# Rows and banks of the state-space stage clear of the last FP4 MLP, and six slots left to the scheduler

## The chip, the cores and the metric

One Trainium2 chip, of which the kernel uses one core. A core has five engines with a queue of instructions each: PE (TensorE, matrix products; its weight loads are told apart as PEld), DVE (VectorE), ACT (ScalarE), POOL (GpSimd) and SP (SyncE, which here issues transfers). They share the on-chip memory SBUF (128 partitions) and the accumulators PSUM (eight banks of 128 x 512 f32). The metric is device time of one launch in microseconds; lower is better.

## The reference

Eight layers, each `x = x + layer(norm(x))`, in four stages of one kernel. Around the change lie the FP4 MLP that ends the first stage and the state-space layers that follow it:

```python
def fp4_quant_dequant(x):           # blocks of 16 along the last dim
    scale = jnp.maximum(jnp.max(jnp.abs(xb), axis=-1, keepdims=True) / 6.0, 1e-12)
    idx = jnp.searchsorted(_MID, jnp.abs(xb / scale))
    q = _GRID[idx] * jnp.sign(xn) * scale
...
gate = fp4_linear(x, w_gate)        # [.., 128] x [352, 128]
y = fp4_linear(x, w_up)
h = jax.nn.silu(gate) * y
return fp4_linear(h, w_down)
```

```python
def mamba_block(x, Wi, cw, cb, Wx, Wdt, bdt, Alog, Dp, Wo):    # 4 layers
    xs, z = jnp.split(x @ Wi.T, 2, axis=-1)
    u = jax.nn.silu(conv(xs, cw) + cb)                        # 4 taps, causal
    dt, Bc, Cc = jnp.split(u @ Wx.T, [8, 24], axis=-1)
    dt = jax.nn.softplus(dt @ Wdt.T + bdt)
    def step(h, inp):                                         # over 256 positions
        dA = jnp.exp(dt_t[:, :, None] * A)                    # 256 channels x 16 states
        h = dA * h + dt_t[:, :, None] * B_t[:, None, :] * u_t[:, :, None]
        y = jnp.einsum('bds,bs->bd', h, C_t)
    ...
    return ((y + u * Dp) * jax.nn.silu(z)) @ Wo.T
```

The 2048 tokens (8 sequences of 256) are worked on in four blocks of 512.

## The kernel before

**Stage l0** runs spiking attention and the FP4 MLP for token blocks 0 to 3, with parts of different blocks woven together. The order of PE's instructions there is the order written in the program; the other engines' order is set by the framework's scheduler. PSUM is cut into banks by use: `mm` 0 to 3, `acc` 4 and 5, `ffn` 6 and 7. SBUF tiles come from pools, of which `fpool` (l0_f) holds the tiles of the MLP and `epool` (l0_e) those of attention's exponentials.

`mlp(tb, lo, hi, kind)` does the token columns lo to hi of a block: quantize the normed input into `xq` (`fp4`: L521 block maxima, L522 and L524 to L525 scale and its inverse, L527 divide, L531 and L532 the exponent's power of two, L534 and L536 rounding by adding and taking off a large number, L538 multiply by the scale; all on DVE, all tiles in SBUF), transpose (L265 on PE, copied by ACT at L268), multiply by gate and up (L722, L729), silu (L725, ACT), product into `h` (L730), quantize `h` into `hq` with the same lines, transpose in three pieces into `hT`, multiply by down (L743) and add to `x` (L746). The last block's MLP is run as two halves side by side, the second seven steps behind the first. The second half's names end in `_2` in the program (the profile cuts numbers off: both are `hq_l0f`, `d_l0f` and so on). It uses the banks of kind `mm`, the first those of kind `ffn`.

**Stage l1a** is the state-space stage. One job is one token block of one layer (4 x 4 jobs), one slot is one of the 16 states of a job: 256 slots. For a slot s:

- `spread` (L995, SP): a DMA that broadcasts two rows of B, or of C, from DRAM to all partitions (512 KB).
- `inflow` (L1001, POOL): `st = du * B row`.
- `decay` (L1007, ACT): `da = exp(dt * A)` into one of two PSUM tiles da0, da1; two instructions a slot.
- `scan` (L1012, DVE): the recurrence along the tokens, `da` from PSUM, `st` in place.
- odd slots: `turn`, four PE transposes (L1021) for each half and on DVE L1028 (slot 1: ACT, L1026) the product with C and the sum into `yt`; even slots: `weigh` (L1034, POOL), `st *= C row`, and a sum on PE (L1043). Slot 8 goes the way of the odd ones.

`front(job)` makes a job's inputs: norm's statistics on DVE (L872, L874) and POOL (L881 to L888), scaled by ACT (L893), transposed (L898), convolution (L909, then L914, silu L917), `xd` (L924, L927), dt (L938, L941, L942), the softplus (L948, L954), z (L964, L966) and DVE's L973 to L976, whose running operand is in PSUM. Its ACT steps switch between function tables (1.28 us a load). `norm(xs[3])` with L238, L240, L246 to L251 and L257 makes `y3`, the last block's input; it needs L746 of both halves.

Job 0's front, the norms and the first part of the job-1 front are given to l0's last steps as `following`. When l0 closes, its pools are freed and l1a's pools are opened in their place: `big` (the rows and the `st` tiles), `pool`, and in PSUM `mm` and `acc` with one bank each, da0, da1 (two banks each) and the sums `y` (two banks). A tile that lies where an older one lay waits for the older one's last reader.

All slots run in a loop `for g in range(len(slots) + 10)` in a `manual_schedule` of PE, DVE, ACT and POOL: these engines take the instructions in the order in which the loop issues them. SP's queue is in order too: the first `spread` holds up all later ones. The code ahead of the loop clears da0 and da1 (L1090, DVE), issues the first rows, three inflows and the first decay.

Of the kernel before, what the change touches and what calls it, by code (L numbers as in the profile page):

```python
# [174 lines left out]
def network_kernel(ctx: ExitStack, tc: tile.TileContext, x_in, packs, places, conv_w, out, stages=STAGES):  # L175
# [16 lines left out]
    def mm_tile(name, kind="mm"):  # L192
        return banks[kind].tile([P, TB], F32, tag=kind, name=name)
# [346 lines left out]
    def l0(w, following):  # L540
        with ExitStack() as es:
# [148 lines left out]
                    A.copy(wT[name], ps[:, :I0P])  # L690
                    yield

            def mlp(tb, lo=0, hi=NT, kind="ffn"):

                n = f"l0f{tb}" + (f"_{lo}" if lo else "")
                more = "2" if lo else ""
                part = range(lo, hi)
                x = xs[tb]

                def whole(tag, shape):  # L700
                    if (tb, tag) not in shared:
                        shared[tb, tag] = fpool.tile(shape, F32, tag=tag, name=f"{tag}_{n}")
                    return shared[tb, tag]

                room = lambda m: flat(whole("q_p", [P, NT, I0P])[:, lo:hi])[:, : (hi - lo) * m]
                if lo == 0:
                    shared[tb, "xn"] = layer_norm(x, n)
                xn = shared[tb, "xn"]
                yield
                xq = whole("xq", [P, NT, D])[:, lo:hi]  # L710
                yield from fp4(fpool, flat(xn[:, lo:hi]), flat(xq), (hi - lo) * D, f"x{n}", room(D), more)
                yield
                yield
                xqT = transposed(xq, n, kind=kind)
                yield
                yield
                h = whole("h", [P, NT, I0P])
                G.memset(h[:, lo:hi, I0:], 0.0)
                g = whole("g", [P, NT, I0])
                for i in part:  # L720
                    pg = mm_tile(f"g_{n}_{i}", kind)
                    T.matmul(pg[:, :I0], xqT[:, ts(i - lo)], wT["gate"][:, :I0], start=True, stop=True)  # L722
                    A.copy(g[:, i, :], pg[:, :I0])
                    yield
                A.activation(g[:, lo:hi], g[:, lo:hi], AF.Silu)  # L725
                yield
                for i in part:
                    pu = mm_tile(f"u_{n}_{i}", kind)
                    T.matmul(pu[:, :I0], xqT[:, ts(i - lo)], wT["up"][:, :I0], start=True, stop=True)  # L729
                    V.tensor_tensor(h[:, i, :I0], g[:, i, :], pu[:, :I0], ALU.mult)  # L730
                    yield
                hq = whole("hq", [P, NT, I0P])[:, lo:hi]
                yield from fp4(fpool, flat(h[:, lo:hi]), flat(hq), (hi - lo) * I0P, f"h{n}", room(I0P), more)
                yield
                yield
                hT = whole("hT", [P, 3, TB])
                for c in range(3):
                    transposed(hq[:, :, ts(c)], f"{n}_{c}", hT[:, c, lo * P : hi * P], kind=kind)
                    yield
                ps = mm_tile(f"d_{n}", kind)  # L740
                for i in part:
                    for c in range(3):
                        T.matmul(ps[:, ts(i)], hT[:, c, ts(i)], wT["down"][:, ts(c)], start=c == 0, stop=c == 2)  # L743
                    yield
                to = flat(x[:, lo:hi])
                V.tensor_tensor(to, to, ps[:, lo * P : hi * P], ALU.add)  # L746
# [28 lines left out]
            with tc.manual_schedule(engines={mybir.EngineType.PE}):  # L775
                for tb in range(2):
                    skip(normal(tb), 4)

                first_half = skip(currents(0), 4 + 10 + 8)
                rest = {}  # L780
                for tb in range(NTB + 1):
                    parts = []
                    if tb < NTB:

                        rest[tb] = attention(tb)
                        parts.append((take(rest[tb], 2 * H), 2 * H + 1))
                    if tb == 0:
                        parts.append((chain(first_half, currents(1), normal(2)), 18 + 40 + 4))
                        parts.append((weights(), 24))
                    elif tb < NTB:  # L790
                        ahead = [currents(tb + 1)] if tb + 1 < NTB else []
                        ahead += [normal(tb + 2)] if tb + 2 < NTB else []
                        if ahead:
                            parts.append((chain(*ahead), 40 + 4))
                    if tb == NTB:
                        last = beside(mlp(tb - 1, 0, NT // 2), mlp(tb - 1, NT // 2, NT, "mm"), 7)
                        parts.append((chain(rest[tb - 1], project(tb - 1), last), 7 + 5 + 36))
                    elif tb:
                        parts.append((chain(rest[tb - 1], project(tb - 1), mlp(tb - 1)), 7 + 5 + 37))

                    if tb >= NTB - 1:
                        n = 2 + 40 + 1 if tb < NTB else 2 + 2 + 1
                        parts.append((take(following, n), n + 1))
                    woven(*parts)


    def l1a(w0):
# [10 lines left out]
        with ExitStack() as es:  # L818
# [215 lines left out]
                G.tensor_tensor(st, st, row.unsqueeze(1).to_broadcast([P, 2, TB]), ALU.mult)  # L1034

            def open_sum(job):
                job.yacc = pda.tile([P, 2, TB], F32, tag="y", name=f"y_{job.n}")
                for c in range(2):
                    T.matmul(job.yacc[:, c, :], diags[job.l][:, c, :], job.u[:, c, :], start=True, stop=False)

# [43 lines left out]
            big = es.enter_context(tc.tile_pool(name="l1a_b", bufs=5))  # L1084
            pool = es.enter_context(tc.tile_pool(name="l1a", bufs=1))
            pda = es.enter_context(tc.tile_pool(name="l1a_da", bufs=1, space=bass.MemoryType.PSUM))

            for j in range(2):
                t = pda.tile([P, 2, TB], F32, tag=f"da{j}", name=f"da{j}")
# [33 lines left out]
                    adds[g - s + ADD[s]] = job, s  # L1123
            gens = {"norm": norm(xs[NTB - 1], f"l1a{NTB - 1}", ys[NTB - 1], gap=3)}
            step = lambda what: next(gens.get(what, iter(())), None)

            kinds = mybir.EngineType
            with tc.manual_schedule(engines={kinds.PE, kinds.DVE, kinds.Activation, kinds.Pool}):
                for g in range(len(slots) + 10):
                    job, s = slot(g)  # L1130

                    nxt = slot(g + LEAD)
                    if nxt[0] and nxt[1] == 0:
                        fronts.append(front(nxt[0]))
                    for gen in fronts:
                        next(gen, None)
                    if job:
                        if s == 0:
                            job.yt = pool.tile([P, NT, DI], F32, tag="yt", name=f"yt_{job.n}", bufs=2)
                            if job.tb == 2 and job.l + 1 < NL:  # L1140
                                gens["weights"] = layer_weights(job.l + 1)

                        rows_of(g + 3 * Q)
                        rows_from(g + 2 * Q)
                    nxt = slot(g + 1)
                    if nxt[0]:
                        decay(*nxt)
                    if slot(g + AHEAD)[0]:
                        inflow(*slot(g + AHEAD))
                    if job:  # L1150
                        scan(job, s)
                    for lag in (1, 2):
                        j2, s2 = slot(g - lag)
                        if j2 and s2 % 2:
                            turn(j2, s2, lag - 1)
                    j2, s2 = slot(g - 2)
                    if j2 and s2 in ADD:
                        weigh(j2, s2)
                    at = g % DS
                    if at in EXTRA:  # L1160
                        j2 = slot(g - DS * EXTRA[at][0])[0]
                        if j2:
                            turn(j2, *EXTRA[at][1:], "mm")
                    if at == 7:
                        step("tail")
                    if job and s == 8:
                        open_sum(job)
                    if g in adds:
                        add_up(*adds[g])
                    for gen in fronts:  # L1170
                        next(gen, None)
                    step("weights")
                    step("norm")
                    if at == 2 and slot(g - DS)[0]:
                        gens["tail"] = tail(slot(g - DS)[0])
                    if 2 < at < 7:
                        step("tail")
                    if g == len(slots) - 1:
                        gate(job.k)

# [440 lines left out]
```

## Time and profile before

| | |
|---|---|
| three runs | 2043.93, 2045.22, 2050.58 us; median 2045.22 |
| the profiled execution | 2052.19 us, its span 2050.4 us |
| busy, share of the span | PE 78%, DVE 79%, POOL 62%, ACT 53%, PE weight loads 46% |
| granted TensorE clock | 0.876 |
| L1012 scans, DVE | 256, 581.5 us, 2277 ns each |
| L1001 inflows, POOL | 256, 597.4 us, 2356 ns each |
| L1034 weighing, POOL | 112, 263.8 us, 2356 ns each |
| L1007 decays, ACT | 512, 351.2 us, 689 ns each |

The state-space stage lies between about 364 and 1345 us. The profile gives times from the start of the span. In the timelines a line is a start, a duration, the engine, the line of the code, the operation, out<-in, and in brackets the idle time before it with what ended it; neighbours of one kind are put together (x4), and their duration runs from the first's start to the last's end. A slice by stage gives each engine's busy time in a stretch. The profiled execution is 6.97 us above the median of the runs.

DVE's waits in the stage (400 to 1330 us): `da` from ACT 35.9 us in 26 waits, L1021 from PE 11.2, L1034 from POOL 2.2. POOL's longest single wait there is the one ahead of the first inflow, 21.43 us.

### The profile page before, as it was taken

The numbers are of one execution on the slowest core, as the hardware profiler recorded it, in microseconds if no ns is written. First come the engines' busy times: TensorE is split into PE (matmuls) and PEld (weight loads), VectorE is DVE, ScalarE is ACT, GpSimd is POOL, SyncE is SP. The second block draws the span as 40 slices with busy tenths as digits, with TensorE's granted clock in tenths as the row PEclk, the third lists the DMA queues.
The fourth block names the chain that finished last, engine by engine and source line by source line (L and its number), as shares of the span: only waits on it lengthen the run. The fifth ranks groups of instructions, "written<-read, shape, count | busy, mean of one in ns | idle before, by whom it ended". The sixth has DMA issues, their size and how long they took to land. (4 is left out here: it accounts for less than half of the span.)

```text
span 2050.4 us, 21148 instructions
## 1 busy us (share of the span) xinstructions
PE 1589.3 (78%) x6829; PEld 947.1 (46%) x6829; DVE 1630.0 (79%) x3009; ACT 1077.4 (53%) x1764; POOL 1266.7 (62%) x920
## 2 busy tenths in 40 slices
PE   4989895587777778877778777789999776794775
PEld 1434443244444444444444343444446575683665
DVE  6775546799999999999999999925655666899996
ACT  2654452676577776667676666522222243463442
POOL 2000101999899998999989999902343545836446
PEclk8999997699888998888898888899999988796887
DMA  4000001433223332233323333100022344220000
GB/s 129 1 1 1 1 2 58 145 107 134 93 105 120 111 125 94 103 115 105 119 103 112 100 112 105 62 1 0 1 74 98 111 150 130 65 72 9 6 6 6
DMA packets 67693, 153.27 MB, mean 75 GB/s; under 512 B 5248, under 2 KB 26368, under 8 KB 67328
## 3 DMA queue, kind: packets, MB, share of 16 engines
q1 hardware_dynamic: 60224, 123.79, 17.9%
q0 software_dynamic: 7360, 28.14, 4.2%
q8 instruction: 54, 0.88, 0.2%
q14 instruction: 55, 0.45, 0.1%
HBM read 142.74 MB, written 9.18 MB: 74 GB/s over the span
## 5 line engine op out<-in xcount | busy, mean ns | idle before, releaser
L1012 DVE TENSOR_TENSOR_SCAN st_l1a<-da,st_l1a 128x1024 f32<-128x1024 f32 x256 | 581.5, 2277 | 49.7 <-ACT da L1007 43.9
L1001 POOL TENSOR_TENSOR st_l1a<-du_l1a,b_l1a 128x1024 f32<-128x1024 f32 x256 | 597.4, 2356 | 21.4 <-DMA b_l1a<-rows_l1a 21.4
L1007 ACT ACTIVATE da<-dt_l1a,na 128x510 f32<-128x510 f32 x512 | 351.2, 689 | 112.9 <-DVE st_l1a L1012 104.2
L1021 PE MATMUL tr_l1a<-w_const,st_l1a 128*128 128x128 f32 x1152 | 201.0, 306 | 185.6 <-DVE yt_l1a L1028 164.2
L1021 PEld LDWEIGHTS tr_l1a<-w_const,st_l1a 128*128 128x128 f32 x1152 | 149.8, 157 | 331.9 <-issue 212.5
L1034 POOL TENSOR_TENSOR st_l1a<-st_l1a,c_l1a 128x1024 f32<-128x1024 f32 x112 | 263.8, 2356 | 60.5 <-DVE st_l1a L1012 60.5
L1043 PE MATMUL y_l1a<-st_l1a,w_const 128*128 128x512 f32 x448 | 243.9, 673 | 0.0
L1028 DVE SCALAR_TENSOR_TENSOR yt_l1a<-tr_l1a,ct_l1a,yt_l1a 128x256 f32<-128x256 f32 x512 | 215.6, 466 | 13.1 <-PE tr_l1a L1021 12.9
L628 PE MATMUL o_l0a<-ex_l0a,va_l0a 128*32 128x256 f32 x512 | 140.6, 401 | 1.9 <-ACT ex_l0a L620 1.9
L909 PE MATMUL u_l1a<-xp,cw 128*128 128x512 f32 x256 | 120.5, 594 | 1.7 <-ACT xp L901 0.9
L1043 PEld LDWEIGHTS y_l1a<-st_l1a,w_const 128*128 128x128 f32 x448 | 88.5, 220 | 66.0 <-issue 66.0
L1235 PE MATMUL h_l1f<-h_l1f,w_l1f 128*128 128x512 f32 x256 | 116.7, 593 | 0.0
L620 ACT ACTIVATE ex_l0a<-s_l0a 128x512 f32<-128x512 f32 x128 | 75.3, 595 | 73.8 <-PE s_l0a L615 73.5
L1508 POOL TENSOR_TENSOR xd<-de,ex_l3f 128x1024 f32<-128x1024 f32 x32 | 65.2, 2056 | 61.1 <-ACT de L1503 61.1
L1543 PE MATMUL wT<-w_const,wa 128*128 128x128 f32 x512 | 73.4, 312 | 22.6 <-ACT wa L1524 17.0
L1239 ACT ACTIVATE h_l1f<-h_l1f,w_l1f 128x512 f32<-128x512 f32 x32 | 22.0, 687 | 120.9 <-PE h_l1f L1235 120.9
L1543 PEld LDWEIGHTS wT<-w_const,wa 128*128 128x128 f32 x512 | 71.1, 226 | 23.9 <-ACT wa L1524 17.4
L1291 POOL TENSOR_TENSOR st_l2a<-st_l2a,qk_l2a 128x512 f32<-128x512 f32 x32 | 40.4, 1268 | 63.1 <-DVE st_l2a L1290 53.6
L1510 POOL TENSOR_TENSOR xd<-xd,ey_l3f 128x1024 f32<-128x1024 f32 x32 | 78.6, 2475 | 0.2
L1235 PEld LDWEIGHTS h_l1f<-h_l1f,w_l1f 128*128 128x128 f32 x256 | 48.6, 190 | 60.2 <-issue 59.2
L386 POOL DMA_INDIRECT we_l2f<-w_l2f,rows_l2f x44 | 45.5, 1034 | 48.5 <-PE y_l2f L419 31.3
L628 PEld LDWEIGHTS o_l0a<-ex_l0a,va_l0a 128*32 128x32 f32 x512 | 47.1, 113 | 59.9 <-issue 34.4
(490 smaller groups left out, 3260.9 us busy)
## 6 DMA issues: line engine op xcount, KB each, us to landing
b_l1a<-rows_l1a SPq DMA_DIRECT2D x128, 512.0 KB, 3.6
c_l1a<-rows_l1a SPq DMA_DIRECT2D x64, 512.0 KB, 4.1
w_l1f<-w_l1f SPq DMA_DIRECT2D x1, 2888.0 KB
in_l2f<-zero SPq DMA_DIRECT2D x4, 704.0 KB, 7.1
w_l1a<-w_l1a SPq DMA_DIRECT2D x4, 572.0 KB, 5.3
cw<-conv_w SPq DMA_DIRECT2D x4, 512.0 KB
xt_l2f<-in_l2f SPq DMA_DIRECT2D x8, 256.0 KB
out_l2f<-yt_l2f SPq DMA_DIRECT2D x8, 256.0 KB, 3.3
```

The costliest lines, as they stand in the source:

```text
L628: T.matmul(po[b, g][32 * j : 32 * j + 32, :S], va[:, 2 * b + kc, h, :], ex[:, ts(kc, S)], start=kc == 0, stop=kc == 1)
L909: T.matmul(seq(ps), cw[:, j, ts(c)], xp[:, :, j : j + S], start=j == 0, stop=j == 3)
L1001: G.tensor_tensor(t, job.du, row.unsqueeze(1).to_broadcast([P, 2, TB]), ALU.mult)
L1007: A.activation(seq(da[:, c, :])[:, :, 1:], seq(job.dt[:, c, :])[:, :, 1:], AF.Exp, scale=rates[job.l][:, k : k + 1])
L1012: V.tensor_tensor_scan(st, flat(das[s % 2]), st, 0.0, ALU.mult, ALU.add)
L1021: T.transpose(ps[:, j * DI + c * P : j * DI + (c + 1) * P], st[:, c, ts(i)], ident)
L1028: V.scalar_tensor_tensor(dst, src, cs, dst, ALU.mult, ALU.add)
L1034: G.tensor_tensor(st, st, row.unsqueeze(1).to_broadcast([P, 2, TB]), ALU.mult)
L1043: T.matmul(job.yacc[:, c, :], ident, job.st[s][:, c, :], start=False, stop=False)
L1235: T.matmul(ps, w(wn)[:, k * HID + c * P : k * HID + (c + 1) * P], h[:, k, :], start=k == 0, stop=k == NC - 1)
L1510: G.tensor_tensor(xd, xd, wide(ey[:, rs].unsqueeze(2), 2, NX, NK), ALU.mult)
L1543: T.matmul(ps[:, ts(c)], wa[:, h, ts(c)], ident, start=h == 0, stop=h == NH - 1)
```

## The change

The second half of the last MLP takes its PSUM tiles from `ffn` instead of `mm`, so both halves share banks 6 and 7. The tile `xq` moves from `fpool` to `epool` (one buffer). The sums `y` get a PSUM pool `py` of their own, opened after `pda`. The loop's body becomes a function `issue(g)`; it is called for slots 0 to 5 ahead of the `manual_schedule` and for the others in it.

```diff
-            def mlp(tb, lo=0, hi=NT, kind="ffn"):
+            def mlp(tb, lo=0, hi=NT):
...
-                def whole(tag, shape):
+                def whole(tag, shape, pool=fpool):
                     if (tb, tag) not in shared:
-                        shared[tb, tag] = fpool.tile(shape, F32, tag=tag, name=f"{tag}_{n}")
+                        shared[tb, tag] = pool.tile(shape, F32, tag=tag, name=f"{tag}_{n}", bufs=1)
                     return shared[tb, tag]
...
-                xq = whole("xq", [P, NT, D])[:, lo:hi]
+                xq = whole("xq", [P, NT, D], epool)[:, lo:hi]
...
-                xqT = transposed(xq, n, kind=kind)
+                xqT = transposed(xq, n, kind="ffn")
...
-                        last = beside(mlp(tb - 1, 0, NT // 2), mlp(tb - 1, NT // 2, NT, "mm"), 7)
+                        last = beside(mlp(tb - 1, 0, NT // 2), mlp(tb - 1, NT // 2, NT), 7)
...
-                job.yacc = pda.tile([P, 2, TB], F32, tag="y", name=f"y_{job.n}")
+                job.yacc = py.tile([P, 2, TB], F32, tag="y", name=f"y_{job.n}")
...
             pda = es.enter_context(tc.tile_pool(name="l1a_da", bufs=1, space=bass.MemoryType.PSUM))
+            py = es.enter_context(tc.tile_pool(name="l1a_py", bufs=1, space=bass.MemoryType.PSUM))
...
+            def issue(g):
+                job, s = slot(g)
+                ...
+
+            for g in range(6):
+                issue(g)
 
             kinds = mybir.EngineType
             with tc.manual_schedule(engines={kinds.PE, kinds.DVE, kinds.Activation, kinds.Pool}):
-                for g in range(len(slots) + 10):
-                    job, s = slot(g)
-                    ...
+                for g in range(6, len(slots) + 10):
+                    issue(g)
```

In the built program this orders the instructions of the boundary so:

- SP: the first row waits for L538 of the second half's `xq`, the transposes of `xq` on PE (L265), the last exponential of attention on ACT and an old POOL instruction. Before, it waited for L538 of `hq`, the last down product (L743), the last copy into `hT` (L268) and POOL's memset (L718).
- DVE: memsets of da and the statistics come ahead of L677; after L522 of the second half stand scan 0, L538 of the first half, L524, scan 1, L525, L527, scan 2, L531, L746 of the first half, L532, L238, L534, L238, L536, two L240, L538, scans 3 to 5, L746 of the second half, scan 6, two L238 and two L240, three pairs of L1028, L872 and L874 of block 2, four L257 of `y3`, scan 7. From scan 7 on the order is that of before.
- POOL: inflows 0 to 5, L1034 of slot 0, inflows 6 to 8, L1034 of slot 2, inflow 9, L1034 of slot 4, inflows 10 and 11, L1034 of slot 6, L246 to L251 for `y3`, inflow 12.
- ACT: silu of job 0's z (L984, with a table load on each side) stands among attention's last exponentials; the decays of slots 0 and 1 ahead of the MLP's first L268; three of the four L893 of job 1 ahead of the second half's L268 of `xq`; the decays of slots 2 to 6 among the copies into `hT`; after the last of these, L914, L1026, L914, L917, L927, L941 and L942 twice, L948, L951, L954, L966 in a row, and then the decay of slot 7.
- PE: one transpose of job 1 (L898) ahead of the second half's transposes of `xq`; the first convolution (L909) ahead of the transposes of `hq`; L1021 of slot 1 among the down products; the second convolution after the last down product, then L924, L938, L947 and L964 with L1021 of slots 3 and 5 between them.

More of the change, by code (lines that the diff above doesn't have):

```diff
@@ L720, in mlp @@
                 for i in part:
-                    pg = mm_tile(f"g_{n}_{i}", kind)
+                    pg = mm_tile(f"g_{n}_{i}", "ffn")
                     T.matmul(pg[:, :I0], xqT[:, ts(i - lo)], wT["gate"][:, :I0], start=True, stop=True)
@@ L727, in mlp @@
                 for i in part:
-                    pu = mm_tile(f"u_{n}_{i}", kind)
+                    pu = mm_tile(f"u_{n}_{i}", "ffn")
                     T.matmul(pu[:, :I0], xqT[:, ts(i - lo)], wT["up"][:, :I0], start=True, stop=True)
@@ L737, in mlp @@
                 for c in range(3):
-                    transposed(hq[:, :, ts(c)], f"{n}_{c}", hT[:, c, lo * P : hi * P], kind=kind)
+                    transposed(hq[:, :, ts(c)], f"{n}_{c}", hT[:, c, lo * P : hi * P], kind="ffn")
                     yield
-                ps = mm_tile(f"d_{n}", kind)
+                ps = mm_tile(f"d_{n}", "ffn")
                 for i in part:
@@ L1125, in l1a @@
             step = lambda what: next(gens.get(what, iter(())), None)
+            def issue(g):
+                job, s = slot(g)
+                nxt = slot(g + LEAD)
+                if nxt[0] and nxt[1] == 0:
+                    fronts.append(front(nxt[0]))
+                for gen in fronts:
+                    next(gen, None)
+                if job:
+                    if s == 0:
+                        job.yt = pool.tile([P, NT, DI], F32, tag="yt", name=f"yt_{job.n}", bufs=2)
+                        if job.tb == 2 and job.l + 1 < NL:
+                            gens["weights"] = layer_weights(job.l + 1)
+                    rows_of(g + 3 * Q)
+                    rows_from(g + 2 * Q)
+                nxt = slot(g + 1)
+                if nxt[0]:
+                    decay(*nxt)
+                if slot(g + AHEAD)[0]:
+                    inflow(*slot(g + AHEAD))
+                if job:
+                    scan(job, s)
+                for lag in (1, 2):
+                    j2, s2 = slot(g - lag)
+                    if j2 and s2 % 2:
+                        turn(j2, s2, lag - 1)
+                j2, s2 = slot(g - 2)
+                if j2 and s2 in ADD:
+                    weigh(j2, s2)
+                at = g % DS
+                if at in EXTRA:
+                    j2 = slot(g - DS * EXTRA[at][0])[0]
+                    if j2:
+                        turn(j2, *EXTRA[at][1:], "mm")
+                if at == 7:
+                    step("tail")
+                if job and s == 8:
+                    open_sum(job)
+                if g in adds:
+                    add_up(*adds[g])
+                for gen in fronts:
+                    next(gen, None)
+                step("weights")
+                step("norm")
+                if at == 2 and slot(g - DS)[0]:
+                    gens["tail"] = tail(slot(g - DS)[0])
+                if 2 < at < 7:
+                    step("tail")
+                if g == len(slots) - 1:
+                    gate(job.k)
@@ L1127, in l1a @@
+            for g in range(6):
+                issue(g)
             kinds = mybir.EngineType
             with tc.manual_schedule(engines={kinds.PE, kinds.DVE, kinds.Activation, kinds.Pool}):
-                for g in range(len(slots) + 10):
-                    job, s = slot(g)
[L1132 to L1179, printed above, removed]
```

## The prediction

> **What bounds the kernel now.** I read the busy shares first, then the slices by stage, then the timelines of VectorE (DVE), GpSimd (POOL) and SyncE's queue around the end of the FP4 MLP, where the change acts. Columns of the slices: the stretch, its length, busy time of PE, PE weight load, DVE, ACT and POOL with their instruction counts, granted clock, DMA share, GB/s.
>
> ```profile
> 333.00:358.00 25.00, 14.51 (x54) 9.94 (x54) 17.20 (x38) 8.39 (x19) 4.42 (x13) 0.71 0.00 0
> 364.00:388.00 24.00, 17.87 (x38) 6.87 (x38) 15.74 (x18) 19.36 (x30) 23.51 (x17) 0.65 0.45 148
> 388.00:402.00 14.00, 4.52 (x11) 2.10 (x10) 14.00 (x18) 7.50 (x10) 14.00 (x7) 0.50 0.34 118
> 402.00:420.00 18.00, 10.72 (x28) 5.77 (x29) 17.79 (x23) 8.84 (x15) 12.86 (x13) 0.72 0.26 88
> 420.00:500.00 80.00, 66.09 (x243) 35.62 (x242) 75.91 (x87) 53.33 (x79) 75.77 (x41) 0.91 0.34 114
> ```
>
> From 388 us on DVE is busy in 14.00 of 14, 17.79 of 18 and 75.91 of 80 us: the 256 slots of the state-space layers run at DVE's pace until about 1345 us. A shift of one slot is therefore carried to the end of the program, unless the 4.1 us idle in the last row take some of it up. The change can win only ahead of slot 7: from 333 to 388 DVE idles for 7.8 us (25.00 less 17.20), 3.9 (358 to 364) and 8.3 (24.00 less 15.74), 20 us in all. That is the ceiling.
>
> ```profile
> 354.24 0.95 DVE L538 TENSOR_TENSOR hq_l0f<-hq_l0f,sc_hl0f 128x768 f32<-128x768 f32 x1
> 357.99 1.28 SPq L995 DMA_DIRECT2D b_l1a<-rows_l1a  x3
> 361.87 13.88 POOL L1001 TENSOR_TENSOR st_l1a<-du_l1a,b_l1a 128x1024 f32<-128x1024 f32 x6 [21.43 <-DMA b_l1a<-rows_l1a]
> 392.40 9.04 DVE L257 TENSOR_SCALAR y<-x,mv_l1a,rs_l1a 128x128 f32<-128x128 f32 x4
> 401.37 2.28 DVE L1012 TENSOR_TENSOR_SCAN st_l1a<-da,st_l1a 128x1024 f32<-128x1024 f32 x1
> ```
>
> These are starts and durations. The MLP's last quantizing product ends at 355.19. The first row transfer is issued at 357.99, after the last down product, since its tile lies where the MLP's were; the first inflow follows 3.88 us later, with POOL idle 21.43 us before it. The line at 401.37 is the scan of slot 7 (slots 0 to 6 start at 364.25, 370.25, 376.30, 378.5, 381.98, 385.40, 388.38).
>
> **What the change moves.** Four edits have one answer, an earlier start: xq out of the MLP's pool, the second half on the banks of the first, a pool of its own for the sums, and the memsets of da ahead. The first row now waits only for the second half's transposes of xq.
>
> - That half is itself later. PE's queue has job 1's transposes ahead of xq's, and these need ACT's L893, which waits for POOL's chain ending at 340.43. Three L893 (1.26 us together) give 341.7, xq's two transposes (0.38) 342.2. So the copy that started at 338.36 moves to 342.5, and the second half's L730 from 343.52 to 345.65: +2.1 us.
> - The row goes out at about 342.25 instead of 357.99; the first inflow starts at 342.25 + 3.88 = 346.1, 15.8 us earlier. The 2888 KB weight load ahead on SP was issued at some 320 and does not compete; before, no DMA moved between 333 and 358.
> - Two memsets (1.82 us) go to about 319, beside ACT's exponentials; da of slots 0 and 1 fills ACT's 13.57 us of idle time before 332.73. The silu of z goes to about 306, with one more table load (1.28 us), and delays the chain to L677 by some 0.7 us, which I leave out; were it not hidden among the exponentials, it would cost 1.04 + 1.28 + 1.28 = 3.6 us.
>
> If nothing else changed, DVE would run the MLP's remainder and three scans together from 345.65: two L730 1.04, L521 0.95, L532 to L538 of the first half 0.56 + 0.96 + 0.96 + 0.89, L522 to L538 of the second 0.19 + 0.44 + 0.17 + 0.96 + 0.56 + 0.56 + 0.96 + 0.96 + 0.95, L746 0.42, statistics 0.63, scans 3 x 2.28: 19.0 us. L538 of the second half would end at about 364.5.
>
> **The price: POOL now runs beside the FP4 arithmetic.** Before, the MLP's DVE work had POOL idle. Now POOL's inflows start at 346.1 and DVE's FP4 operations (L527, L531, L532, L534, L536, L538; all in SBUF, mostly two inputs) lie in the same 30 us. What that costs, rows of the trace tell:
>
> ```profile
> 394.43 4.63 POOL L1001 TENSOR_TENSOR st_l1a<-du_l1a,b_l1a 128x1024 f32<-128x1024 f32 x2
> 410.81 0.70 DVE L974 SCALAR_TENSOR_TENSOR one_l1a<-one_l1a,du_l1a 128x512 f32<-128x512 f32 x1
> 406.76 6.97 POOL L1001 TENSOR_TENSOR st_l1a<-du_l1a,b_l1a 128x1024 f32<-128x1024 f32 x3
> 519.85 5.74 DVE L849 TENSOR_TENSOR cw<-cw,w_l1a 128x1024 f32<-128x1024 f32 x1
> 519.84 2.35 POOL L1034 TENSOR_TENSOR st_l1a<-st_l1a,c_l1a 128x1024 f32<-128x1024 f32 x1
> 522.16 2.34 POOL L1001 TENSOR_TENSOR st_l1a<-du_l1a,b_l1a 128x1024 f32<-128x1024 f32 x1
> ```
>
> L257 takes 0.34 us with POOL idle; the four at 392.40 take 9.04, each ending just after a POOL product. L849 takes 1.21 us alone and 5.74 here, through two POOL products. L974, with its first operand in PSUM, stays at 0.70 beside POOL, and so do the scans (da in PSUM) at 2.28. So an operation with its inputs in SBUF stands still until POOL's running one ends, or longer.
>
> The walk, with one POOL product per such operation (L257's row): POOL has 12 products (inflows 0 to 9, L1034 of slots 0 and 2) before it waits for scan 4, which is behind the MLP. 346.1 + 12 x 2.35 = 374.3; in between POOL lets ten DVE operations pass (0.56, 0.95, 0.95, 0.2, 0.9, 0.2, 0.95, 0.56, 0.56, 0.95: 6.8); after it DVE still does L536, statistics and L538, 2.4. L538 ends at 383.5. If instead an operation waits out a whole unbroken run (L849's row): inflows 0 to 5 to 360.0, then L534 to scan 0, a run of four products to 374.5, and so on: 389.5. The lower bound is 364.5. I take 385, near the first, since four L257 in a row lost one product each.
>
> The Trainium skill's page "SBUF — State Buffer" (section "Who interferes with whom") speaks against this change: two SBUF inputs contend with GpSimd, and whoever issues first holds the shared ports for the whole instruction, no more. By that the wait is one product and the end 383.5; L849's two products say it can be more. The sums here go by the rows.
>
> **From there to slot 7.** In the new ACT order slot 7's decay stands behind the whole front of job 1, which before lay between slots 1 and 6. From L538's end: transposes, three copies, scan 3, its decay and the down products, 5.0 (before: 355.19 to 357.86, plus scan 3); L914 0.69; four convolution matmuls 3.70 at the clock of 0.50; L914 0.69; table and silu 2.34; xd 1.80 and copy 0.58; dt and L941/L942 twice 2 x (1.04 + 1.37); L948 with table 2.34; ct 0.19; L954 with table 2.34; z 0.57; table and decay 2.69: 27.8 us; at full PE clock 25. DVE's own queue (L1028 three pairs, statistics, the L257s) ends near 410.5 and does not decide. Slot 7 starts at 385 + 28 = 413 instead of 401.37: +11.6 us. The first seven slots are early (scan 0 by about 6 us even so), but it is given back.
>
> Profiled execution: 2050.4 + 11.6 = 2062 of span and 1.8 outside. The three runs have a median of 2045.22, 7 us under the profiled one (2052.19); on that scale 2045.2 + 11.6 = 2056.8.
>
> **Rivals.**
> 1. No contention of note: FP4 operations stay at 0.55 to 0.96 us. L538 at 364.5, slot 7 at 364.5 + 25 to 29.7, so 390 to 394, 7 to 11 us earlier: 2034 to 2038. For it: scans and L974 are untouched. Against: L257, L849. It decides if the wait per operation is under 0.6 us (7.4 us over 12). Chance 0.25. This is the other side.
> 2. About half a product of wait (1.15 us for nine operations): L538 at 375, slot 7 at 403: 2047, no change. It needs POOL held up by row transfers. Chance 0.16.
> 3. DVE waits out whole runs: L538 at 389.5, slot 7 at 418 to 419: 2062 to 2063. For it: L849. Chance 0.12.
> 4. The row is not issued earlier (some other tile keeps SP's queue): scan 0 at 364 and slot 7 at about 402: 2046. Against: no such wait is left in the program. Chance 0.04.
> The forecast has 0.43.
>
> **Numbers.** About 0.3% (6 us) is what a measurement of this kernel can tell from no change. Rival 1 is faster (0.25), rivals 2 and 4 are the same (0.20), forecast and rival 3 are slower (0.55). The range of the likeliest alone is 2051 to 2063. The range for all reaches down into rival 1 and up over rival 3: 2036 to 2065.
>
> **What would show it.** The first inflow at about 346; FP4 operations between 346 and 385 with 1 to 4 us in place of 0.55 to 0.96, their ends on POOL's; L538 of the second half ending near 385; slot 7 near 413 behind L1007, itself behind L954. If those durations are short, the forecast falls and rival 1 holds. If slot 7 is late but later stretches hold fewer idle us, my carrying of the shift to the end is wrong.

## The result: 0.6% slower, and the profile after

| | before | after |
|---|---|---|
| runs | 6, median 2047.36 us (2042.13 to 2053.07) | 6, median 2058.35 us (2055.43 to 2065.55) |
| ratio, 95% interval | | 1.0062 (1.0046 to 1.0077) |
| the profiled execution | 2052.19 us, span 2050.4 | 2055.43 us, span 2053.7 |

The medians lie 11.0 us apart, the profiled executions only 3.2: that of before was 5 us above its median, that of after 3 us below. Scan 7 is 11.8 us later in this pair of profiles, scan 16 still 11.8, the last scan 7.5. Executions of one kernel differ by some 10 us, so the size is read from the medians and the place from the profiles.

The slices of the changed kernel, with the columns of those of before:

```profile
333.00:358.00 25.00, 14.38 (x31) 7.10 (x30) 18.07 (x30) 9.13 (x15) 15.90 (x19) 0.77 0.37 126
364.00:388.00 24.00, 8.64 (x35) 7.19 (x34) 23.96 (x18) 7.25 (x14) 17.73 (x8) 0.57 0.33 111
388.00:402.00 14.00, 10.07 (x27) 3.98 (x26) 4.38 (x9) 5.71 (x9) 11.00 (x10) 0.87 0.02 6
402.00:420.00 18.00, 12.11 (x26) 5.24 (x25) 9.68 (x22) 13.79 (x19) 9.41 (x11) 0.50 0.35 116
420.00:500.00 80.00, 62.23 (x229) 33.62 (x228) 76.84 (x91) 51.64 (x81) 66.75 (x36) 0.90 0.29 101
```

POOL is now busy 15.90 of the first 25 us where it was 4.42, as meant. DVE counts as full from 364 to 388 (23.96 of 24, before 15.74), and after that it stands idle for 9.6 of 14 and 8.3 of 18 us. The timelines of DVE and POOL tell why (start, duration, engine, line). First four FP4 operations of the kernel before, with POOL idle, then the changed kernel:

```profile
344.86 0.56 DVE L532 TENSOR_SCALAR q_p_l0f<-q_p_l0f 128x768 f32<-128x768 f32 x1
...
346.19 0.95 DVE L534 SCALAR_TENSOR_TENSOR hq_l0f<-q_p_l0f,hq_l0f 128x768 f32<-128x768 f32 x1
...
349.43 0.96 DVE L527 TENSOR_TENSOR hq_l0f<-h_l0f,rs_hl0f 128x768 f32<-128x768 f32 x1
...
351.61 0.96 DVE L534 SCALAR_TENSOR_TENSOR hq_l0f<-q_p_l0f,hq_l0f 128x768 f32<-128x768 f32 x1
```

```profile
346.95 0.52 DVE L730 TENSOR_TENSOR h_l0f<-g_l0f,u_l0f 128x352 f32<-128x352 f32 x1 [3.48 <-ACT g_l0f L725]
347.39 2.29 DVE L532 TENSOR_SCALAR q_p_l0f<-q_p_l0f 128x768 f32<-128x768 f32 x1
...
350.03 2.67 DVE L534 SCALAR_TENSOR_TENSOR hq_l0f<-q_p_l0f,hq_l0f 128x768 f32<-128x768 f32 x1
...
365.63 3.03 DVE L527 TENSOR_TENSOR hq_l0f<-h_l0f,rs_hl0f 128x768 f32<-128x768 f32 x1
...
374.06 2.89 DVE L534 SCALAR_TENSOR_TENSOR hq_l0f<-q_p_l0f,hq_l0f 128x768 f32<-128x768 f32 x1
...
380.04 0.92 DVE L538 TENSOR_TENSOR hq_l0f<-hq_l0f,sc_hl0f 128x768 f32<-128x768 f32 x1
...
413.15 2.29 DVE L1012 TENSOR_TENSOR_SCAN st_l1a<-da,st_l1a 128x1024 f32<-128x1024 f32 x1 [5.36 <-ACT da L1007]
```

```profile
346.92 16.32 POOL L1001 TENSOR_TENSOR st_l1a<-du_l1a,b_l1a 128x1024 f32<-128x1024 f32 x6 [5.97 <-ACT g_l0f L725]
363.20 2.35 POOL L1034 TENSOR_TENSOR st_l1a<-st_l1a,c_l1a 128x1024 f32<-128x1024 f32 x1
365.51 8.01 POOL L1001 TENSOR_TENSOR st_l1a<-du_l1a,b_l1a 128x1024 f32<-128x1024 f32 x3
```

Both engines lose: six inflows take 16.32 us instead of 13.88, and nine FP4 operations of DVE hold 2.13 to 3.03 us each: L532 2.29, L534 2.67, L536 2.23, L522 2.32, L525 2.13, L527 3.03, then L532 2.37, L534 2.89, L536 2.89. With POOL idle the same shapes take 0.56, 0.96, 0.96, 0.18, 0.17, 0.96, 0.56, 0.96 and 0.96. The difference is 16.6 us. The last L538 ends at 380.96 (before 355.19), slot 7 starts at 413.15 (401.37).

### The profile page after: what moved, and what is told of

It is laid out like the page before. It is cut to its first block, busy times and chain, and to the rows that moved or that the text cites. A ratio compares the mean times of both kernels' runs of the same rounds, so it can differ in the third digit from the quotient of the medians.

```text
span 2053.7 us, 21142 instructions
## 1 busy us (share of the span) xinstructions
PE 1589.8 (77%) x6829; PEld 951.4 (46%) x6829; DVE 1634.1 (80%) x3009; ACT 1080.9 (53%) x1766; POOL 1270.4 (62%) x920
## 5 line engine op out<-in xcount | busy, mean ns | idle before, releaser
L1021 PE MATMUL tr_l1a<-w_const,st_l1a 128*128 128x128 f32 x1152 | 199.5, 304 | 173.6 <-DVE yt_l1a L1028 150.4
L1034 POOL TENSOR_TENSOR st_l1a<-st_l1a,c_l1a 128x1024 f32<-128x1024 f32 x112 | 264.8, 2364 | 71.0 <-DVE st_l1a L1012 71.0
L1021 PEld LDWEIGHTS tr_l1a<-w_const,st_l1a 128*128 128x128 f32 x1152 | 149.0, 156 | 316.7 <-issue 207.6
L1028 DVE SCALAR_TENSOR_TENSOR yt_l1a<-tr_l1a,ct_l1a,yt_l1a 128x256 f32<-128x256 f32 x512 | 216.3, 469 | 24.7 <-PE tr_l1a L1021 15.9
L909 PE MATMUL u_l1a<-xp,cw 128*128 128x512 f32 x256 | 122.6, 602 | 2.0 <-ACT u_l1a L914 1.1
```

The source lines that it names most:

```text
L909: T.matmul(seq(ps), cw[:, j, ts(c)], xp[:, :, j : j + S], start=j == 0, stop=j == 3)
L1021: T.transpose(ps[:, j * DI + c * P : j * DI + (c + 1) * P], st[:, c, ts(i)], ident)
L1028: V.scalar_tensor_tensor(dst, src, cs, dst, ALU.mult, ALU.add)
```

## The experiments

Ratios are to the kernel before, run on the same chip. Since the same work stands up to 3 us apart in whole profiles (the first half's first L730 starts between 337.46 and 340.45), two distances inside each are given too: from the start of the first half's first L730 to the end of the last L538, and to the scan of slot 7 (before: 16.7 and 62.9 us).

| kernel | median, us | ratio (95%) | to the last L538 | to slot 7 |
|---|---|---|---|---|
| the change | 2058.35 | 1.0062 (1.0046 to 1.0077) | 42.0 | 74.1 |
| all slots in the loop's order | 2059.05 | 1.0054 (1.0039 to 1.0069) | 34.0 | 75.6 |
| slots to the scheduler alone | 2045.62 | 0.9996 (0.9984 to 1.0007) | 16.6 | 60.9 |
| POOL reads added to before | 2052.62 | 1.0027 (1.0015 to 1.0039) | 22.4 | 68.6 |
| POOL memsets added to before | 2046.61 | 0.9995 (0.9986 to 1.0004) | 16.8 | 61.6 |
| the change, few columns read | 2042.76 | 0.9982 (0.9967 to 0.9997) | 25.3 | 57.3 |
| before, L849 on POOL | 2039.17 | 0.9963 (0.9950 to 0.9975) | 16.7 | 61.3 |
| slots, y3 on ACT, L849 on POOL | 2034.60 | 0.9942 (0.9926 to 0.9958) | 16.6 | 57.2 |
| the change with these two moves | 2054.98 | 1.0039 (1.0026 to 1.0052) | 42.4 | 74.5 |

The median of before beside these was 2047.36, 2047.26 (second to fifth row) and 2046.59 us (the last four).

**One part of the change at a time.** First the rows and banks of the change, with no slot left to the scheduler:

```diff
-            for g in range(6):
-                issue(g)
...
-                for g in range(6, len(slots) + 10):
+                for g in range(len(slots) + 10):
                     issue(g)
```

> The changed kernel with all slots in the order written in the loop (banks and rows of the change kept). Theory A (POOL's early inflows hold up the FP4 arithmetic, and this alone makes the loss): the first inflow still starts near 347, six inflows lie beside the FP4 operations, L538 of the second half ends near 372 instead of 355, slot 7 starts at 408 to 414, 7 to 13 us slower than before. Theory B (the loss is the front of job 1 standing in one row ahead of slot 7's decay, which this undoes): slot 7 within 4 us of 401.4, no change against before.

Theory A holds: L538 ends at 374.4 and slot 7 starts at 416.04 by this profile, which runs 1.9 us behind that of before (372.5 and 414.1 on its time), and the loss is that of the whole change. The DVE timeline:

```profile
371.33 0.95 DVE L534 SCALAR_TENSOR_TENSOR hq_l0f<-q_p_l0f,hq_l0f 128x768 f32<-128x768 f32 x1
...
373.46 0.94 DVE L538 TENSOR_TENSOR hq_l0f<-hq_l0f,sc_hl0f 128x768 f32<-128x768 f32 x1
...
388.80 2.29 DVE L1012 TENSOR_TENSOR_SCAN st_l1a<-da,st_l1a 128x1024 f32<-128x1024 f32 x1 [8.52 <-ACT da L1007]
...
416.04 2.28 DVE L1012 TENSOR_TENSOR_SCAN st_l1a<-da,st_l1a 128x1024 f32<-128x1024 f32 x1
```

The MLP is through earlier here than in the change: POOL stops after seven inflows, where it waits 10.30 us for DVE's L240, and again after the eighth, 12.04 us for scan 2; so L534 and L538 are back at 0.95. But scan 1 itself (388.80) now waits for ACT behind the MLP's end, so the slots have nothing in hand, and slot 7 comes just as late. So what the scheduler's six slots gained and lost comes out even.

Then the other part alone, with the rows, pools and banks of before:

```diff
-                for g in range(len(slots) + 10):
-                    ...
+            for g in range(6):
+                issue(g)
...
+                for g in range(6, len(slots) + 10):
+                    issue(g)
```

> The kernel before with only slots 0 to 5 left to the scheduler (rows, banks and pools as before). Theory A: FP4 operations keep 0.55 to 0.96 us, L538 of the second half ends near 355, slots 0 to 6 follow the inflows at 2.3 us each, slot 7 starts at 392 to 397 instead of 401.4: 4 to 9 us faster than before. Theory B: the front in one row makes slot 7 late, at 406 or later, 5 us slower or more.

The FP4 operations do stay short, and theory B is out, but the gain is 0.8 us by the ratio (1.6 by the medians) and not 4 to 9: by the interval, 3.3 faster to 1.4 slower, no change that can be told from noise. DVE's timeline shows what took it:

```profile
365.03 11.52 DVE L1012 TENSOR_TENSOR_SCAN st_l1a<-da,st_l1a 128x1024 f32<-128x1024 f32 x5 [3.67 <-POOL st_l1a L1001]
380.40 2.29 DVE L1012 TENSOR_TENSOR_SCAN st_l1a<-da,st_l1a 128x1024 f32<-128x1024 f32 x1 [3.85 <-ACT da L1007]
...
392.18 7.51 DVE L257 TENSOR_SCALAR y<-x,mv_l1a,rs_l1a 128x128 f32<-128x128 f32 x4
399.61 2.27 DVE L1012 TENSOR_TENSOR_SCAN st_l1a<-da,st_l1a 128x1024 f32<-128x1024 f32 x1
```

Five scans run without a break, and scan 4 starts 7.7 us earlier than in the profile before; then scan 5 waits for ACT, and the four L257 of y3 stand 7.51 us behind POOL's products ahead of slot 7. They begin no earlier than in the profile before (392.40), since all three L1028 pairs now stand between scan 6 and them (before, one did) and two of these wait for PE (1.34 and 1.27 us): that is what I had not counted.

**The collision by itself.** The kernel before has POOL idle beside the last MLP. Thirteen products on a scratch tile fill that time; the orders of DVE, ACT and PE are those of before, instruction by instruction:

```diff
+                if tb == NTB - 1 and not lo:
+                    dummy = epool.tile([P, TB], F32, tag="ex", name="dummy")
+                    G.memset(dummy, 0.0)
+                    G.tensor_tensor(dummy[:, :I0], h[:, 0, :I0], h[:, 0, :I0], ALU.mult)
+                    for k in range(12):
+                        G.tensor_tensor(dummy, dummy, dummy, ALU.mult)
```

> The kernel before with 13 extra POOL products on a scratch tile in SBUF (12 of 128x512, some 1.25 us each, from about 341 us) in POOL's idle time beside the last FP4 MLP; the orders of the other engines are unchanged and nobody waits for them. Theory A: FP4 operations of DVE grow by up to 1.25 us each, L538 of the second half ends 8 to 13 us later, the program 8 to 13 us slower. Theory B (no contention that matters): unchanged within 3 us.

Nobody waits for these products, and yet the program is 5.4 us slower (2052.62 against 2047.26). In the profile, the products on POOL and two of DVE's lines:

```profile
342.77 18.82 POOL L737 TENSOR_TENSOR dummy<-dummy 128x512 f32<-128x512 f32 x12
...
357.31 1.68 DVE L534 SCALAR_TENSOR_TENSOR hq_l0f<-q_p_l0f,hq_l0f 128x768 f32<-128x768 f32 x1
...
360.95 1.46 DVE L538 TENSOR_TENSOR hq_l0f<-hq_l0f,sc_hl0f 128x768 f32<-128x768 f32 x1
```

L534 takes 1.68 instead of 0.96. The size was over-estimated: 5.7 us to the last L538, not 8 to 13, because each operation waits for the rest of one product only, and some find POOL between two (L527 0.96 in both halves, the first half's L534 and L536 0.94). The twin of this run puts memsets in place of the twelve products:

```diff
-                        G.tensor_tensor(dummy, dummy, dummy, ALU.mult)
+                        G.memset(dummy, 0.0)
```

> The same with the 12 products replaced by memsets of the same tile, which read nothing. Theory A: FP4 operations keep 0.55 to 0.96 us and the time is that of before within 3 us, since only POOL's reads collide; if writes collide too, some 3 to 8 us slower. Theory B: unchanged within 3 us.

```profile
340.23 7.58 POOL L737 MEMSET dummy<- 128x512 f32 x12
...
345.22 0.94 DVE L534 SCALAR_TENSOR_TENSOR hq_l0f<-q_p_l0f,hq_l0f 128x768 f32<-128x768 f32 x1
346.09 0.60 DVE L522 TENSOR_SCALAR sc_hl0f<-sc_hl0f 128x48 f32<-128x48 f32 x1
```

No change in time. L534 beside a memset keeps 0.94. The memsets are shorter (most 0.53 us, 7.58 together), so this run covers six of the twelve operations and not all; in those it is the reading that makes the two-input operations wait.

**The change without the reads.** In the changed kernel the inflows of slots 0 to 9 become a memset and a product of 8 of the 512 columns, the weighing of slots 0 and 2 a product of 8 columns; the rest of these states is left at zero or unweighed. DVE, ACT and PE keep the order of the changed kernel.

```diff
...
+                if job.k == 0 and s < 10:
+                    G.memset(t, 0.0)
+                    t, row = t[:, :, :8], row[:, :8]
+                    G.tensor_tensor(t, job.du[:, :, :8], row.unsqueeze(1).to_broadcast([P, 2, 8]), ALU.mult)
...
```

> The changed kernel with the long reads of POOL taken out beside the FP4 MLP: inflows of slots 0 to 9 become a memset of the tile and a product of 8 of 512 columns, the weighing of slots 0 and 2 a product of 8 columns; the orders of DVE, ACT and PE stay those of the changed kernel. Theory A (POOL's reads hold up the FP4 arithmetic and that is the loss): FP4 operations back at 0.55 to 0.96 us, L538 of the second half ends at 364 to 366 instead of 381, slot 7, which stood 32 us behind it, starts near 397: 3 to 8 us faster than before, 14 to 19 us faster than the change. Theory B (the order around the boundary is the loss, not the contention): slot 7 stays at 408 or later and the time within 4 us of the change's.

This is the run that settles it: 3.8 us faster than before (2042.76 against 2046.59), though the same order with full reads is 11 us slower. Its runs spread more than those of the others: eight lie between 2037.14 and 2044.62, four between 2049.18 and 2050.33, and the profile is of one of these four; by the interval the gain is 0.6 to 6.8 us. DVE's timeline (the scan is L1017 in this file):

```profile
362.80 0.93 DVE L534 SCALAR_TENSOR_TENSOR hq_l0f<-q_p_l0f,hq_l0f 128x768 f32<-128x768 f32 x1
...
364.87 0.92 DVE L538 TENSOR_TENSOR hq_l0f<-hq_l0f,sc_hl0f 128x768 f32<-128x768 f32 x1
...
397.78 2.29 DVE L1017 TENSOR_TENSOR_SCAN st_l1a<-da,st_l1a 128x1024 f32<-128x1024 f32 x1 [5.36 <-ACT da L1012]
```

From the first L730 to the last L538 it takes 25.3 us instead of 42.0: 16.6 us less, the sum of the nine waits above. The memsets are shorter than the inflows (0.95 us instead of 2.35), so POOL's time shrinks with its reads; but operations with two SBUF inputs that stand right beside a memset take 0.93 to 0.95 us (L534 and L538 of the first half), so it is the reads that had held them. From there to slot 7 it is 32.0 us, in the change 32.2.

**Toward a faster kernel.** The same collision stands in the kernel before: L849 three times, and L257 ahead of slot 7. Three runs move these away, the first in one line:

```diff
-                V.tensor_tensor(cw, cw, w(f"wx{l}").unsqueeze(1).to_broadcast([P, 4, DI]), ALU.mult)
+                (G if l else V).tensor_tensor(cw, cw, w(f"wx{l}").unsqueeze(1).to_broadcast([P, 4, DI]), ALU.mult)
```

> The kernel before with one line of another engine: the product of the convolution's weights (L849) of layers 1 to 3 on POOL instead of DVE. In the profile before it took DVE 5.74, 4.86 and 5.80 us behind POOL's products. Theory A: DVE, which sets the pace there, is rid of up to 16 us and POOL, which waits for DVE, has room for 3 products of 2.4 us: 9 to 16 us faster. Theory B (POOL is as tight as DVE): within 4 us of before.

7.4 us faster, 1.6 under what was expected at the least. On POOL the product takes one product's time; the timeline of POOL:

```profile
512.32 2.35 POOL L849 TENSOR_TENSOR cw<-cw,w_l1a 128x1024 f32<-128x1024 f32 x1
```

DVE had spent 16.4 us on the three. Its waits from 400 to 1330 us grow: 18.0 us for PE's transposes in place of 11.2, 37.1 for `da` in place of 35.9.

```profile
DVE st_l1a L1012 <- ACT da L1007: 37.1, 29, 2.3
DVE yt_l1a L1028 <- PE tr_l1a L1021: 18.0, 19, 3.2
```

These waits take back 8.0 of the 16.4 us. That does not close the sum: the last scan stands 14.1 us earlier than in the profile before, which was 5 us above its median, and the medians give 7.4.

The second and third run add the last step of y3's norm on ACT (two more tiny operations on POOL give the shift), on top of the slots alone and of the whole change:

```diff
...
-            V.tensor_scalar(dst[:, i, :], src[:, i, :], mv[:, i, 0:1], rstd[:, i : i + 1], ALU.subtract, ALU.mult)
+            A.activation(dst[:, i, :], src[:, i, :], AF.Identity, bias=t[:, i : i + 1], scale=rstd[:, i : i + 1])
...
```

> The kernel before with slots 0 to 5 left to the scheduler, the last step of y3's norm (four L257, 7.5 us behind POOL's products where it takes 1.1 us alone) on ACT, and L849 of layers 1 to 3 on POOL. Theory A: slot 7 at about 395 (the decay sets it) instead of 401, and 9 to 16 us from L849: 13 to 21 us faster than before. Theory B: no more than 4 us.

> The changed kernel with the same two moves (y3's last step on ACT, L849 on POOL). Theory A: the FP4 MLP is held up as in the change, slot 7 stays at about 411 to 415, and L849 gives 9 to 16 us: within 5 us of before, and some 13 to 20 us slower than the kernel with the two moves and the rows as before.

The slots with both moves are 12.0 us faster than before, a little less than expected, and the fastest kernel here: slot 7 starts at 395.82 and waits for its decay, as forecast. The rows of the change with both moves are 8.4 us slower than before and 20.4 slower than that, where I had allowed for 5 and 13 to 20: slot 7 is at 414.52 behind the held-up MLP. So the early rows cost more in the better kernel: 17.3 us at slot 7 and 20.4 in the medians, where the change alone cost 11.2 and 11.0.

## Why the prediction was right, and where its sizes were off

- **The bound.** The shift at slot 7 is carried in the main: 11.8 us at slots 7, 8 and 16 of the profiles, 11.0 in the medians (forecast 11.6). That the last scan is only 7.5 us later lies in part in the profile before, whose execution was a long one: against the profile of the kernel with memsets, which is as fast as before and was taken at 2046.96 us, slot 7 is 12.6 us later and the last scan 10.6, both counted from the first L730.
- **The earlier start** came within 1.3 us of what was worked out, in a profile that itself runs 0.5 us behind that of before: first row at 342.57 (342.25), second half's first L730 at 346.95 (345.65), first inflow at 346.92 (346.1).
- **The price.** One POOL product for each operation (L257's row) gave 383.5, whole runs (L849's row) 389.5, and I took 385; measured 380.96. The first row was the right one, and still a little high: 16.6 us against 19.0, since L538 and L531 found POOL between two products. L849's longer wait did not come back here; in the profile before it spans two POOL products, and why it does when these did not was not tried. The few-columns run shows the cause: with the reads gone the last L538 ends 25.3 us behind the first L730, where the walk without contention had 26.0 (364.5 less 338.49).
- **From there to slot 7** the forecast had 27.8 us, and it was 32.2. What was mis-sized is PE's work at the clock that it got, most of all the four convolution matmuls, "3.70 at the clock of 0.50" (eight records in the profile). The row of 3.70 us that I used was at a granted clock of 1.00, not 0.50. The first slice is of before and holds the convolution, the second is of after and holds the same; the third, of after, holds the second matmul of the dt step (L938):

```profile
359.90:363.70 3.80, 3.70 (x8) 1.43 (x8) 0.76 (x1) 2.68 (x4) 1.83 (x1) 1.00 0.96 345
```

```profile
387.40:393.20 5.80, 5.76 (x10) 2.53 (x11) 3.23 (x7) 0.71 (x2) 5.80 (x4) 0.64 0.00 0
401.70:403.80 2.10, 2.04 (x3) 0.54 (x4) 0.28 (x1) 0.01 (x1) 0.00 (x0) 0.54 0.81 219
```

  3.70 / 0.64 is 5.78, the 5.76 that was measured: 2.1 us more. PE had waited 13.84 us for L538 before; whether that is why its clock was lower was not tried. The second L938 took 2.02 us where I had 1.04: 1.0 more. The way from L538 to the first L914 took 5.8 us instead of 5.0 (the transposes 1.81 instead of 0.88), and between the second L914 and the silu stands an L1026 (0.47) that I had not counted. This error and that of the price are of one size and opposite, so slot 7 was met to 0.2 us (413 against 413.15) with more luck than the terms deserved.
- **Rival 1** (no contention) would have been 3.8 us faster by the few-columns run (0.6 to 6.8), not 7 to 11: the chain to slot 7 is longer than I had it.
- **Theory B of the experiments**, that the front of job 1 in one row ahead of slot 7 is the loss, is out: with the loop's order the loss is the same, and with the scheduler's order without the early rows there is none.

## What to carry to other kernels

Before an idle GpSimd is given earlier work, look at what VectorE does in that stretch: operations that read SBUF twice (here 0.96 us became 2.2 to 3.0), and the `tensor_scalar` forms that read it once (0.56 became 2.3, 0.18 became 2.3), can each wait for a running GpSimd product, and the work gained on one engine is taken from the other. Here inflows that came 15 us early held up by 16.6 us a chain that everything behind it needed. An idle stretch of one engine beside the critical chain of another may be what keeps that chain fast.

## What the runs showed of the hardware

- Beside POOL's products in the changed kernel, DVE's L521 (a reduction of one SBUF tile) kept 0.94 us and the scans, with `da` in PSUM, 2.22 to 2.28.
- A POOL memset leaves DVE's two-input operations alone (L534 0.94 beside it), but collides with its `tensor_scalar` ones: L522 took 0.60 us instead of 0.18 there, and in the few-columns run, beside memsets of 128x1024, L531 1.04 instead of 0.56. It can be the memset that waits: beside L531 and L532, which kept 0.59 and 0.55, two memsets took 0.82 and 0.83 us instead of 0.53. The Trainium skill's page "SBUF — State Buffer" (section "Who interferes with whom") has two rules that fit: two SBUF inputs contend with a GpSimd instruction that reads SBUF and not with one that only writes it, and the two-port modes, which `tensor_scalar` can enter, contend with GpSimd as such.
- In a POOL stream that is kept waiting, the POOL operations grow too: six inflows 16.32 us instead of 13.88, beside FP4 operations of 0.96 us.
- In these rows the duration of f32 matmuls went as one over the granted clock (the convolution 3.70 us at 1.00 and 5.76 at 0.64, L938 1.12 at 1.00 and 2.02 at 0.54). A row's duration is of use only with the clock of its own slice.
